# Windowed attention in blocks of 32 queries by 64 keys, with the mask added on VectorE and the maximum subtracted on GpSimd

## The chip, the cores and the metric

The kernel runs on one core of a Trainium2 chip. A core has five engines with queues of their own: TensorE (PE; its weight loads are shown as PEld), VectorE (DVE), ScalarE (ACT), GpSimd (POOL) and SyncE (SP), which here issues the transfers. Each engine takes its instructions in the order in which the program lists them, and waits where one needs another engine's result. The metric is the device time of one execution in microseconds (us).

## The reference

There are two parts, one after the other, for a batch of 8 sequences of 512 tokens with 128 features. The first part is one layer of causal attention with 16 heads of 8 features, whose weights are found by four Newton steps. It is not touched by the change.

The second part has six layers. Each computes queries, keys and values for 16 heads of 64 features, scales queries and keys to unit length, rotates them, and lets each query attend to its own window of 32 tokens and the 32 before it:

```python
mask = (it < jb) | (it > jb + w) | (jb == -1)          # w = 32
sim = jnp.einsum('bhwie,bhwje->bhwij', bq, bk2) * QK_SCALE
sim = jnp.where(mask, -jnp.finfo(sim.dtype).max, sim)
attn = jax.nn.softmax(sim, -1)
out = jnp.einsum('bhwij,bhwje->bhwie', attn, bv2)
```

The heads are joined by `Wo` and added to the input; a feed-forward block with layer norm, two projections, a GELU gate and a projection back follows, and is added too.

## The kernel before

All arithmetic is in float32. The second part is one long pipeline over *halves*: a half is one layer, one sequence and 8 of the 16 heads, and there are 6 × 8 × 2 = 96 of them. A half has four *pairs* of heads, so the loop `while t < ...` makes 384 steps of one pair each, with a few more at the ends. One step `t` of the loop holds work of several stages:

- `turn(a)` (L570) transposes the rotated queries and keys of pair `t` on PE, so that features lie on partitions; ACT copies them to `qT`.
- `share` (L614) sums the exponentials of the pair before over the keys (DVE, `rs`, L618), takes the reciprocal (L619), and multiplies by it on POOL (L620).
- `turn_weights` (L624) transposes the weights of the pair two steps back on PE, and ACT copies them to `prT` (L631).
- `prepare_qk` (L511) makes queries and keys for one quarter of the next half: the projection `m` on PE (L518), its squares on ACT (L523) and their sums `ss` on DVE (L524), and the rotation: two products on DVE (L526, L534), an add on POOL (L538), and after the reciprocal root of `ss` on ACT (L542, L543) a multiplication on POOL (L546).
- `weigh(a)` (L585) makes the scores of pair `t` and their exponentials; it is what the change rewrites.
- `gather` (L633) multiplies the weights of the pair two steps back with the values on PE (`po`), and ACT copies the result to `oT` (L647); `leave` (L649) multiplies it with `wo` into `acc`.
- `prepare_v` (L550) makes a quarter of the next half's values, which ACT copies into `v` (L558); after the fourth quarter `spread` (L560) moves `v` by transfers within on-chip memory to `v3`, where the keys of each query block lie on partitions.

In eight steps of two halves, the feed-forward block of one sequence runs in pieces between the stages: `gp` (L703), `ap` (L713) and `y` (L724) are its three groups of matmuls, and the GELU (L664) needs two loads of a function table around it.

In `weigh` a block has 64 queries and 96 keys. Two PE matmuls per pair (L592) first write the mask `band`, held in bfloat16, into PSUM with an identity matrix; 16 score matmuls (L601) add to it, in tiles of 64 rows by 64 columns. DVE takes the negative maximum (L607) and adds it (L608), for each of the two heads apart, straight from PSUM; ACT takes exp of both (L612). The weights of a pair are 128 partitions by 768 numbers.

The order of the instructions on each engine is made when the program is built, by a scheduler with a model of times; the engines keep to it. Buffers come from pools: `ps_a` has four PSUM banks that rotate through transposes, projections and the feed-forward block, `ps_b` two for the scores, `ps_c` one each for `po` and `acc`. `v` has one buffer, `v3` and most others two, `pr` three.

Of the kernel before, what the change touches and what calls it, by code (L numbers as in the profile page):

```python
# [16 lines left out]
P = 128  # L17
N = 512
# [14 lines left out]
WIN = 32  # L33
QB = 64
KB = QB + WIN
NQ = N // QB
HH = H // 2
HC = HH * DHL
# [11 lines left out]
def tile_kernel(  # L50
# [26 lines left out]
    make_identity(nc, ident)  # L77
    ident_h = const.tile([P, P], BF16, name="ident_h")
    nc.gpsimd.tensor_copy(ident_h, ident)
    eps_ln = const.tile([P, 1], F32, name="eps_ln")  # L80
# [349 lines left out]
    nc.gpsimd.memset(band[0:QB, 0, 0:WIN], NEG)  # L430

# [128 lines left out]
    def spread(g):  # L560

        v, v3 = g["v"], g["v3"]
        nc.gpsimd.memset(v3[0:WIN, 0, :], 0.0)
        for u in range(2):
# [20 lines left out]
    def weigh(a):  # L585

        qT = a["qT"]
        a["pr"] = pr = tp.tile([P, 2, NT, KB], F32, name="pr", bufs=3)
        nm = tp.tile([P, 2, NT], F32, name="nm")
        s = [ps_b.tile([P, NT, KB], F32, name="s2") for e in range(2)]  # L590
        for e in range(2):
            nc.tensor.matmul(  # L592
                s[e].rearrange("p c k -> p (c k)"), lhsT=ident_h,
                rhs=band.rearrange("p c k -> p (c k)"), start=True, stop=False,
            )
        for n in range(NQ):
            c, u = n // 2, n % 2
            k0 = max(n * QB - WIN, 0)
            for e in range(2):
                hr = slice(e * DHL, (e + 1) * DHL)  # L600
                nc.tensor.matmul(  # L601
                    s[e][u * QB : (u + 1) * QB, c, KB - (n + 1) * QB + k0 : KB],
                    lhsT=qT[0][hr, n * QB : (n + 1) * QB], rhs=qT[1][hr, k0 : (n + 1) * QB],
                    start=False, stop=(n >= NQ - 2),
                )
        for e in range(2):
            nc.vector.tensor_reduce(nm[:, e], s[e], axis=AX.X, op=ALU.max, negate=True)  # L607
            nc.vector.tensor_tensor(  # L608
                pr[:, e], s[e], nm[:, e].unsqueeze(2).to_broadcast([P, NT, KB]), ALU.add
            )  # L610
        flat = pr.rearrange("p e c k -> p (e c) k")
        nc.scalar.activation(flat, flat, AF.Exp)  # L612

    def share(a):  # L614

        flat = a["pr"].rearrange("p e c k -> p (e c) k")
        rs = tp.tile([P, 2 * NT], F32, name="rs")
# [5 lines left out]

    def turn_weights(a):  # L624
        pr = a["pr"]
        a["prT"] = prT = tp.tile([KB, 2, NT, P], F32, name="prT")
        for e in range(2):
            pT = ps_a.tile([KB, NT, P], F32, name="pT2", tag="mm")
            for c in range(NT):
                nc.tensor.transpose(pT[:, c, :], pr[:, e, c, :], ident)  # L630
            nc.scalar.copy(prT[:, e], pT)  # L631

    def gather(a):  # L633

        g, p, prT = a["g"], a["p"], a["prT"]
        po = ps_c.tile([P, N], F32, name="po2")
        for n in range(NQ):
            for e in range(2):
                h = 2 * p + e
                nc.tensor.matmul(  # L640
                    po[e * DHL : (e + 1) * DHL, n * QB : (n + 1) * QB],
                    lhsT=g["v3"][:, n, h * DHL : (h + 1) * DHL],
                    rhs=prT[:, e, n // 2, (n % 2) * QB : (n % 2 + 1) * QB],
                    start=True, stop=True,
                )
# [222 lines left out]
```

## Time and profile before

| quantity | value |
| --- | --- |
| median of three runs | 5278.99 us (5274.19 to 5279.23) |
| profiled execution | 5272.88 us |
| its span | 5271.2 us, so 1.7 us lie around it |
| DVE busy over the span | 4459.5 us (85%) |
| PE busy over the span | 4383.2 us (83%) |
| ACT busy over the span | 3831.5 us (73%) |
| POOL busy over the span | 3207.5 us (61%) |
| mean granted PE clock | 0.883 of full speed |

In a row of the profile, a group of instructions is named by its line, engine, operation, and tiles as `out<-in`; `x` gives how many there were, followed by busy time and mean length. A timeline row gives start, length, engine, line and tiles, and in brackets how long the engine stood idle before it and what ended the wait. In a row of the view by stretches, the stretch and its length come first, then busy time and number of instructions of PE, PEld, DVE, ACT and POOL, the granted PE clock, the share of time in which the transfer engines were busy, and GB/s. In the chain that ended last, each row has a start, a length and what the chain ran through; a chain that stays on one engine means that nothing else set the pace there.

### The profile page before, as it was taken

To read this page: it belongs to the slowest core of one execution; us is meant where nothing else is said; L and a number is where in the kernel's file an instruction comes from. 1 tells how busy PE (TensorE), PEld (TensorE's weight loads), DVE (VectorE), ACT (ScalarE), POOL (GpSimd) and SP (SyncE) were. 2 spreads that over 40 slices of the span, in tenths; PEclk is the share of its full clock that TensorE was granted. 3 is DMA by queue.
4 is the path that set the end of the run, shared out by engine and by line. 5 is a ranking of instruction groups with operands and counts; after the bars stand their busy time and mean duration, and the time that the engine had idled before them with its cause. 6 is when DMAs were issued, how large, how long until landed. Compare 5 with 4: busy or idle time off the path is not lost.

```text
span 5271.2 us, 116180 instructions
## 1 busy us (share of the span) xinstructions
PE 4383.2 (83%) x44173; PEld 2609.3 (50%) x44173; DVE 4459.5 (85%) x11788; ACT 3831.5 (73%) x6698; POOL 3207.5 (61%) x3919
## 2 busy tenths in 40 slices
PE   4555556556554799999999999999999999999998
PEld 1222222223222466666666666666666666666665
DVE  7888888888887788888888888888888888888886
ACT  6899888888889466666666666666666666666665
POOL 2444434444445677777777767777777777677674
PEclk7666666666665899999999999999999999999999
DMA  0000000000000211221112212121122112121221
GB/s 9 1 5 1 5 5 1 5 3 3 3 1 3 68 47 38 50 53 46 47 41 58 50 37 51 48 53 46 37 50 61 40 46 49 44 57 46 49 55 36
DMA packets 115043, 177.87 MB, mean 34 GB/s; under 512 B 13072, under 2 KB 38456, under 8 KB 114488
## 3 DMA queue, kind: packets, MB, share of 16 engines
q1 hardware_dynamic: 114488, 170.45, 13.0%
q8 instruction: 351, 5.75, 0.5%
q14 instruction: 204, 1.67, 0.1%
HBM read 21.52 MB, written 4.19 MB: 5 GB/s over the span
## 4 chain that ended last, share of the span: by engine, by line
DVE 40%; PE 33%; ACT 17%; POOL 6%; issue 3%; DMA 0%; SPq 0%; ACTq 0%; POOLq 0%; DVEq 0%
DVE stw L285 7%; DVE qr L534 6%; DVE ss L524 5%; PE m L518 5%; DVE qn L526 5%; ACT d L283 4%; ACT d L282 3%; DVE rs L618 3%; PE po L640 3%; PE pv L554 3%; PE pT L630 3%; PE acc L653 3%; PE s L601 2%; PE s L242 2%; PE y L724 2%
## 5 line engine op out<-in xcount | busy, mean ns | idle before, releaser
L538 POOL TENSOR_TENSOR qn<-qn,qr 128x512 f32<-128x512 f32 x768 | 974.5, 1269 | 458.9 <-DVE qr L534 326.3
L620 POOL TENSOR_TENSOR pr<-pr,rs 128x768 f32<-128x768 f32 x384 | 564.1, 1469 | 503.3 <-DVE rs L619 255.2
L285 DVE BATCH_NORM_STATS2 stw<-d 128x6 f32<-128x224 f32 (+15 forms) x2048 | 770.1, 427 | 115.9 <-ACT d L283 114.9
L257 POOL TENSOR_TENSOR d<-ns,lam 128x32 f32<-128x32 f32 (+7 forms) x1024 | 401.4, 426 | 729.3 <-DVE stw L285 229.6
L546 POOL TENSOR_TENSOR qn<-qn,ss 128x512 f32<-128x512 f32 x768 | 784.5, 1042 | 56.3 <-ACT ss L543 56.2
L518 PE MATMUL m<-wqkv,xs 128*128 128x512 f32 x1536 | 750.0, 606 | 79.6 <-ACT qT L582 67.8
L524 DVE TENSOR_REDUCE ss<-sq 128x8 f32<-128x512 f32 x768 | 521.2, 679 | 256.7 <-ACT sq L523 254.9
L282 ACT ACTIVATE d<-ns,lam 128x416 f32<-128x416 f32 (+7 forms) x1024 | 566.8, 614 | 36.6 <-DVE stw L285 14.8
L534 DVE TENSOR_TENSOR qr<-m,tab 128x256 f32<-128x256 f32 x1536 | 570.6, 412 | 0.0
L647 ACT COPY oT<-po 128x512 f32<-128x512 f32 x384 | 223.9, 583 | 461.3 <-PE po L640 461.2
L283 ACT ACTIVATE d<-d 128x1344 f32<-128x1344 f32 (+3 forms) x512 | 551.4, 1095 | 0.2
L242 PE MATMUL s<-kn,qj 32*32 32x352 f32 (+15 forms) x4096 | 422.5, 519 | 151.4 <-DVE mn L247 148.5
L526 DVE TENSOR_TENSOR qn<-m,tab 128x512 f32<-128x512 f32 x768 | 513.9, 669 | 0.0
L618 DVE TENSOR_REDUCE rs<-pr 128x8 f32<-128x768 f32 x384 | 363.6, 947 | 171.8 <-ACT pr L612 171.6
L323 PE MATMUL dTp<-ident,da 128*128 128x128 f32 x1280 | 303.2, 377 | 243.8 <-issue 95.7
L523 ACT ACTIVATE sq<-m 128x512 f32<-128x512 f32 x768 | 433.8, 602 | 82.7 <-PE m L518 67.7
L582 ACT COPY qT<-ptq 128x512 f32<-128x512 f32 x768 | 414.0, 583 | 83.8 <-PE ptq L577 78.8
L257 POOL TENSOR_TENSOR da<-ns,lam 128x416 f32<-128x416 f32 (+15 forms) x512 | 310.4, 639 | 259.2 <-PE dTp L323 229.0
L577 PEld LDWEIGHTS ptq<-ident,qn 128*128 128x128 f32 x3072 | 359.0, 141 | 219.4 <-issue 112.0
L640 PE MATMUL po<-prT,v 96*64 96x64 f32 x12288 | 443.2, 225 | 0.1
L631 ACT COPY prT<-pT 96x512 f32<-96x512 f32 x768 | 427.9, 587 | 13.2 <-PE pT L630 7.7
L554 PE MATMUL pv<-wqkv,xs 128*128 128x512 f32 x768 | 432.2, 645 | 0.9 <-PE m L518 0.7
(137 smaller groups left out, 8785.2 us busy)
## 6 DMA issues: line engine op xcount, KB each, us to landing
v<-v SPq DMA_DIRECT2D x192, 512.0 KB
v<-v SPq DMA_DIRECT2D x96, 256.0 KB
v<-v SPq DMA_DIRECT2D x96, 192.0 KB
wqkv<-in_L_ffn_Wqkv_dram SPq DMA_DIRECT2D x36, 256.0 KB
wo<-in_L_ffn_Wo_dram SPq DMA_DIRECT2D x12, 256.0 KB
xb<-in_L_attn_x_dram SPq DMA_DIRECT2D x8, 256.0 KB
x<-xb SPq DMA_DIRECT2D x8, 256.0 KB
xr<-x SPq DMA_DIRECT2D x8, 256.0 KB
```

Source lines behind the costliest of these rows:

```text
L257: nc.gpsimd.tensor_tensor(o, n, by.to_broadcast([P, keys(W, a)]), ALU.add)
L282: nc.scalar.activation(dv[a], nv[a], AF.Ln, bias=lam[:, c : c + 1])
L283: nc.scalar.activation(d, d, AF.Exp, scale=-1.0)
L285: nc.vector.bn_stats(st[:, 4 * j + a].rearrange("p u k -> p (u k)"), dv[a])
L518: nc.tensor.matmul(m.rearrange("p h e -> p (h e)"), lhsT=lhsT, rhs=wqkv[:, t, :], start=True, stop=True,)
L524: nc.vector.tensor_reduce(ss[:, t, :], sq, axis=AX.X, op=ALU.add)
L526: nc.vector.tensor_tensor(qc, m, tab[:, 2 * t, c, :].unsqueeze(1).to_broadcast([P, HH, DHL]), ALU.mult)
L534: nc.vector.tensor_tensor(qr[:, :, u, :], mh[:, :, 1 - u, :], sw.unsqueeze(1).to_broadcast([P, HH, hd]), ALU.mult,)
L538: nc.gpsimd.tensor_tensor(qc, qc, qr.rearrange("p h u e -> p h (u e)"), ALU.add)
L546: nc.gpsimd.tensor_tensor(qc, qc, ss[:, t, :].unsqueeze(2).to_broadcast([P, HH, DHL]), ALU.mult)
L554: nc.tensor.matmul(pv, lhsT=lhsT, rhs=wqkv[:, 2, :], start=True, stop=True,)
L640: nc.tensor.matmul(po[e * DHL : (e + 1) * DHL, n * QB : (n + 1) * QB], lhsT=g["v3"][:, n, h * DHL : (h + 1) * DHL], rhs=prT[:, e, n // 2, ...
```

## The change

A block now has 32 queries and 64 keys, and the scores of both heads of a pair lie in one PSUM tile of two banks. The mask no longer passes through PE: DVE adds `band`, now float32, to the scores as it moves them out of PSUM, for both heads in one instruction, and takes the maximum from the result; POOL adds the negative maximum. The first block of a sequence has 64 keys too, of which the mask takes away those that lie ahead, so `band` is built differently for it.

The two heads' weights lie side by side, 2 × 64 keys, so that one PE transpose of 128 columns turns both: four transposes and one ACT copy per pair instead of eight and two. The score matmuls have tiles of 64 rows by 32 columns and 64 keys, 32 of them per pair instead of 16. `gather` multiplies 64 keys with 32 queries, 32 matmuls per pair instead of 16, one head on the lower and one on the upper half of the partitions. So `v3` is laid out anew, and `spread` has 18 transfers in place of 4; the value columns of `wqkv` are loaded in an order that puts even heads first, with two transfers in place of one.

```diff
-QB = 64
+QB = 32
 KB = QB + WIN
 NQ = N // QB
+UB = P // QB
...
-    ident_h = const.tile([P, P], BF16, name="ident_h")
-    nc.gpsimd.tensor_copy(ident_h, ident)
...
-    ps_b = ctx.enter_context(tc.tile_pool(name="ps_b", bufs=2, space=PSUM))
+    ps_b = ctx.enter_context(tc.tile_pool(name="ps_b", bufs=1, space=PSUM))
...
-    band = k2.tile([P, NT, KB], BF16, name="band")
+    band = k2.tile([P, NT, KB], F32, name="band")
...
-    nc.gpsimd.memset(band[0:QB, 0, 0:WIN], NEG)
+    nc.gpsimd.memset(band[0:QB, 0], 0.0)
+    nc.gpsimd.affine_select(
+        out=band[0:QB, 0], in_=band[0:QB, 0], pattern=[[-1, KB]], base=0,
+        channel_multiplier=1, compare_op=ALU.is_ge, fill=NEG,
+    )
...
-        for k in range(3):
+        for k in range(2):
             c0 = k * INNER + hv * HC
             nc.sync.dma_start(w[:, k, :], f_wqkv[l][:, c0 : c0 + HC])
+
+        c0 = 2 * INNER + hv * HC
+        cols = f_wqkv[l][:, c0 : c0 + HC].rearrange("i (p e d) -> i e p d", e=2, d=DHL)
+        for e in range(2):
+            nc.sync.dma_start(
+                w[:, 2, e * (HC // 2) : (e + 1) * (HC // 2)].rearrange("i (p d) -> i p d", d=DHL),
+                cols[:, e],
+            )
...
-        v3 = vp.tile([KB, NQ, HC], F32, name="v3")
+        v3 = vp.tile([P, NQ, HC // 2], F32, name="v3")
...
     def spread(g):
         v, v3 = g["v"], g["v3"]
-        nc.gpsimd.memset(v3[0:WIN, 0, :], 0.0)
-        for u in range(2):
-            nc.sync.dma_start(v3[WIN:KB, u::2, :], v[u * QB : (u + 1) * QB])
-        nc.sync.dma_start(v3[0:WIN, 1::2, :], v[QB - WIN : QB])
-        nc.sync.dma_start(v3[0:WIN, 2::2, :], v[P - WIN : P, 0 : NT - 1])
+        for e in range(2):
+            at = slice(e * KB, e * KB + WIN)
+            cols = slice(e * (HC // 2), (e + 1) * (HC // 2))
+            for u in range(UB):
+                own = v[u * QB : (u + 1) * QB, :, cols]
+                c = 1 if u == 0 else 0
+                nc.sync.dma_start(v3[e * KB + WIN : (e + 1) * KB, u + c * UB :: UB, :], own[:, c:])
+                if u < UB - 1:
+                    nc.sync.dma_start(v3[at, u + 1 :: UB, :], own)
+                else:
+                    nc.sync.dma_start(v3[at, UB::UB, :], own[:, 0 : NT - 1])
+            nc.sync.dma_start(v3[e * KB : (e + 1) * KB, 0, :], v[0:KB, 0, cols])
...
     def weigh(a):
         qT = a["qT"]
-        a["pr"] = pr = tp.tile([P, 2, NT, KB], F32, name="pr", bufs=3)
-        nm = tp.tile([P, 2, NT], F32, name="nm")
-        s = [ps_b.tile([P, NT, KB], F32, name="s2") for e in range(2)]
-        for e in range(2):
-            nc.tensor.matmul(
-                s[e].rearrange("p c k -> p (c k)"), lhsT=ident_h,
-                rhs=band.rearrange("p c k -> p (c k)"), start=True, stop=False,
-            )
+        a["pr"] = pr = tp.tile([P, NT, 2, KB], F32, name="pr", bufs=3)
+        nm = tp.tile([P, NT * 2], F32, name="nm")
+        both = ps_b.tile([P, 2, N], F32, name="s2")
+        s = both[:, :, 0 : NT * KB].rearrange("p e (c k) -> p e c k", c=NT)
         for n in range(NQ):
-            c, u = n // 2, n % 2
+            c, u = n // UB, n % UB
...
-                    s[e][u * QB : (u + 1) * QB, c, KB - (n + 1) * QB + k0 : KB],
-                    lhsT=qT[0][hr, n * QB : (n + 1) * QB], rhs=qT[1][hr, k0 : (n + 1) * QB],
-                    start=False, stop=(n >= NQ - 2),
-                )
-        for e in range(2):
-            nc.vector.tensor_reduce(nm[:, e], s[e], axis=AX.X, op=ALU.max, negate=True)
-            nc.vector.tensor_tensor(
-                pr[:, e], s[e], nm[:, e].unsqueeze(2).to_broadcast([P, NT, KB]), ALU.add
-            )
-        flat = pr.rearrange("p e c k -> p (e c) k")
+                    s[u * QB : (u + 1) * QB, e, c, :],
+                    lhsT=qT[0][hr, n * QB : (n + 1) * QB], rhs=qT[1][hr, k0 : k0 + KB],
+                    start=True, stop=True,
+                )
+        nc.vector.tensor_tensor(
+            pr.rearrange("p c e k -> p e c k"), s,
+            band.unsqueeze(1).to_broadcast([P, 2, NT, KB]), ALU.add,
+        )
+        flat = pr.rearrange("p c e k -> p (c e) k")
+        nc.vector.tensor_reduce(nm, flat, axis=AX.X, op=ALU.max, negate=True)
+        nc.gpsimd.tensor_tensor(
+            flat, flat, nm.unsqueeze(2).to_broadcast([P, 2 * NT, KB]), ALU.add
+        )
         nc.scalar.activation(flat, flat, AF.Exp)
...
     def turn_weights(a):
         pr = a["pr"]
-        a["prT"] = prT = tp.tile([KB, 2, NT, P], F32, name="prT")
-        for e in range(2):
-            pT = ps_a.tile([KB, NT, P], F32, name="pT2", tag="mm")
-            for c in range(NT):
-                nc.tensor.transpose(pT[:, c, :], pr[:, e, c, :], ident)
-            nc.scalar.copy(prT[:, e], pT)
+        a["prT"] = prT = tp.tile([P, NT, P], F32, name="prT")
+        pT = ps_a.tile([P, NT, P], F32, name="pT2", tag="mm")
+        for c in range(NT):
+            nc.tensor.transpose(pT[:, c, :], pr[:, c].rearrange("p e k -> p (e k)"), ident)
+        nc.scalar.copy(prT, pT)

     def gather(a):
...
         for n in range(NQ):
+            c, u = n // UB, n % UB
             for e in range(2):
-                h = 2 * p + e
+                rows = slice(e * KB, (e + 1) * KB)
                 nc.tensor.matmul(
                     po[e * DHL : (e + 1) * DHL, n * QB : (n + 1) * QB],
-                    lhsT=g["v3"][:, n, h * DHL : (h + 1) * DHL],
-                    rhs=prT[:, e, n // 2, (n % 2) * QB : (n % 2 + 1) * QB],
+                    lhsT=g["v3"][rows, n, p * DHL : (p + 1) * DHL],
+                    rhs=prT[rows, c, u * QB : (u + 1) * QB],
                     start=True, stop=True,
                 )
```

More of the change, by code (lines that the diff above doesn't have):

```diff
@@ L562, in spread @@
         v, v3 = g["v"], g["v3"]
-        nc.gpsimd.memset(v3[0:WIN, 0, :], 0.0)
-        for u in range(2):
-            nc.sync.dma_start(v3[WIN:KB, u::2, :], v[u * QB : (u + 1) * QB])
-        nc.sync.dma_start(v3[0:WIN, 1::2, :], v[QB - WIN : QB])
-        nc.sync.dma_start(v3[0:WIN, 2::2, :], v[P - WIN : P, 0 : NT - 1])
+        for e in range(2):
+            at = slice(e * KB, e * KB + WIN)
+            cols = slice(e * (HC // 2), (e + 1) * (HC // 2))
+            for u in range(UB):
+                own = v[u * QB : (u + 1) * QB, :, cols]
[6 more added lines that the diff above has]
+            nc.sync.dma_start(v3[e * KB : (e + 1) * KB, 0, :], v[0:KB, 0, cols])
     def turn(a):
@@ L601, in weigh @@
                 nc.tensor.matmul(
[L602 to L611 removed]
+                    s[u * QB : (u + 1) * QB, e, c, :],
+                    lhsT=qT[0][hr, n * QB : (n + 1) * QB], rhs=qT[1][hr, k0 : k0 + KB],
+                    start=True, stop=True,
+                )
+        nc.vector.tensor_tensor(
[7 more added lines that the diff above has]
+        )
         nc.scalar.activation(flat, flat, AF.Exp)
     def share(a):
[L616 removed]
+        flat = a["pr"].rearrange("p c e k -> p (c e) k")
         rs = tp.tile([P, 2 * NT], F32, name="rs")
```

## The prediction

> **What bounds the kernel now.** I read the page first, then the second part by stretches, then the chain that ended last, then one step engine by engine. The change touches only the second part (about 1790 us to the end).
>
> ```profile
> PE 4383.2 (83%) x44173; PEld 2609.3 (50%) x44173; DVE 4459.5 (85%) x11788; ACT 3831.5 (73%) x6698; POOL 3207.5 (61%) x3919
> ```
> ```profile
> 400.00:800.00 400.00, 227.41 (x1936) 112.26 (x1936) 333.50 (x1191) 353.17 (x509) 166.84 (x366) 0.65 0.01 4
> ...
> 3000.00:5000.00 2000.00, 1952.54 (x20604) 1219.04 (x20603) 1741.07 (x3875) 1342.82 (x2619) 1421.83 (x1324) 1.00 0.19 48
> ```
> The page's averages mix two parts. In the second (last row), PE is busy 98%, DVE 87%, POOL 71%, ACT 67%, and the clock is full. Exp of L612 runs 342 times between 2100.3 and 5196.6 us, so one head pair (a "step") takes 3096.3/341 = 9.08 us.
>
> ```profile
> 3508.12 1.72 PE m L518 x4
> 3509.84 0.33 PE s L592 x2
> 3510.17 0.82 PE s L601 x32
> 3510.99 1.08 PE po L640 x32
> 3512.07 1.05 PE pv L554 x2
> 3513.12 2.58 PE y L724 x6
> 3515.70 0.86 PE acc L653 x2
> 3516.56 0.87 PE ptq L577 x8
> 3517.44 0.87 PE pT L630 x8
> ```
> The chain stays on PE for long stretches. Without feed-forward a step's PE work is 1.72+.33+.82+1.08+1.05+.86+.87+.87 = 7.6 us; `gp`, `ap`, `y` add 2.58 us in three steps of eight.
>
> A second loop lies just under it. Here are DVE's row sum and rotation, then its softmax work after them, then POOL and ACT beside it, from the timeline of one step without the 2.58 us matmuls (start, length):
> ```profile
> 3534.70 0.95 DVE L618 TENSOR_REDUCE rs<-pr 128x8 f32<-128x768 f32 x1 [0.97 <-ACT pr L612]
> 3535.67 0.69 DVE L524 TENSOR_REDUCE ss<-sq 128x8 f32<-128x512 f32 x1
> ...
> 3538.79 0.74 DVE L534 TENSOR_TENSOR qr<-m,tab 128x256 f32<-128x256 f32 x2
> ```
> ```profile
> 3539.52 1.01 DVE L607 TENSOR_REDUCE nm<-s 128x4 f32<-128x384 f32 x2
> 3540.45 1.01 DVE L608 TENSOR_TENSOR pr<-s,nm 128x384 f32<-128x384 f32 x2
> ...
> 3542.43 0.95 DVE L618 TENSOR_REDUCE rs<-pr 128x8 f32<-128x768 f32 x1
> ```
> ```profile
> 3539.67 1.27 POOL L538 TENSOR_TENSOR qn<-qn,qr 128x512 f32<-128x512 f32 x1 [0.37 <-DVE ss L541]
> 3540.91 2.04 POOL L546 TENSOR_TENSOR qn<-qn,ss 128x512 f32<-128x512 f32 x2
> ```
> ```profile
> 3541.56 0.84 ACT L612 ACTIVATE pr<-pr 128x768 f32<-128x768 f32 x1 [0.19 <-DVE pr L608]
> ```
> Call x the end of the last rotation product (3538.79+.74 = 3539.53). Then: subtraction ends x+1.93, exp ends x+2.87, the row sum `rs` starts x+2.90. `rs` stands in DVE's order ahead of the next step's rotation, and from `rs` to the next x is 3539.53−3534.70 = 4.83 us. Period 7.73 us: DVE and ACT go round in about PE's time, and POOL is not in this loop.
>
> **The change, part by part.** The kept rows give the prices; PE first, per step.
>
> *Mask matmuls* go: −.33. *Weight transposes* go from 8 to 4 of 128 columns at .109: −.43. *Scores*: 32 instructions on four tiles take .82; 64 on eight tiles, each tile 8 of 64 columns. Eight turns of 64/96 of today's .10 are about .55, plus start: .63, so −.19. If 64 cost what each of 32 costs now (25.6 ns): 1.64, +.82. *Gather*: 32 instructions, two tiles side by side, 1.08. Afterwards 64, moving 32 columns instead of 64, with weights of 64 columns as before. Weight loads average 133 ns for 64 columns (L601) and 190 for 128 (L518), .89 ns a column, so 64 columns need 57 ns, while 32 moving columns need 32 × .85 = 27 ns. The loads no longer hide: 32 turns × 57 + .15 = 1.97, +.89. Ends: hidden all the same 1.04 (−.04), or 64 at today's 33.7 ns, 2.16 (+1.08). PE sum: −.06 us a step, between −.99 and +1.14. Work on PE is about unchanged; matmuls are not where the time moves.
>
> *DVE* loses two reductions and two subtractions (1.93 together), gains an add from PSUM of 512 (as L526, .67, in steady turn .60) and a reduction (as L524, .68, in turn .60); row sum 768 to 512 saves .35. *ACT*: one copy of .58 goes, exp 768 to 512 takes about .60 (L523's 602 ns). *POOL* gains a broadcast subtraction of 128x512, the form of L546 (1042 ns), and its weighting falls from 1469 to 1042; the memset of .51 per half goes. POOL: about 6.45−.43−.13+1.04 = 6.9 us a step, not full.
>
> But the loop now passes through POOL, whose order in the built program is `qn`+`qr` twice, `qn`×`ss` twice, then the subtraction, then the weighting; only a few steps differ. From the rows above: second add x+.14, multiplications x+1.38 to x+3.42, subtraction x+3.38 to x+4.42. Mask add and maximum are done on DVE at x+1.3 and wait for nothing; the 2.0 us of multiplications, until now beside the loop, stand in it. Exp ends x+5.11, `rs` starts x+5.14; from `rs` to the next x 4.83−.35 = 4.48. What waits behind the subtraction on POOL, the weighting and the next adds, is not needed before the next x. Period **9.6 us** against PE's 7.6.
>
> ACT's order adds to it. Behind the waiting exp stand, in about 26% of steps, nothing that matters (9.61); in 36% the copy of `prT` (.48 in turn), which puts `ss` .37 behind the end of the row sum (9.98); in 26% both `qT` copies and `prT` (three × .48): exp ends x+5.11, `sq` to x+7.2, then 3.75 of DVE: 10.95; in 12% also the copy of `v`: 11.45. DVE cannot start `ss` without `sq`, nor PE the scores without `qT`. In one step of eight the copies of `xf` (.60+.61) stand before the subtraction: +1.24/8. Mean: .26×9.61+.36×9.98+.26×10.95+.12×11.45+.155 = 10.47 us. Feed-forward steps (PE 10.2) coincide with the late-exp ones and fit in them, and DVE's extra work there fits into its wait from x+1.3 to x+5.14.
>
> The subtraction against a page: the Trainium skill, "GPSIMD Engine Reference", section 3.1, has GpSimd taking 1.96 times as long as VectorE on a two-input add. Against the .67 of L526 that estimate gives 1.31 for the subtraction, .27 more a step, +104 us; the row of the same form here has 1042 ns, and the sum goes by the row.
>
> *Spread of v*: 18 transfers a half instead of 4, 2.0 MB instead of 1.5. Fourteen are issued after the last chunk of `v`, at the .62 to .67 us of L565 and L567: 9.8 us, and 2.5 more until the last lands. The next half's first copy into the single buffer `v` waits for it, and ACT behind it. Today that copy starts 11.8 to 13.0 us after the last; in the built order it stands one step with GELU or three steps later (16 us and more). So 0; without that cover up to 3 us × 48 = 144. `v3` is wanted four steps later. The split `wqkv` loads (12 in all) have five steps. The larger band is built once: +0 to 5 us. The scores keep two PSUM banks, single buffered as now, and give them back after one DVE add (x+.7) instead of after the second subtraction (x+1.9): no cost. A bank of the pool of four is held while a chunk of `v` waits for its copy, two steps at most in every other half; the transposes need one bank less a step, so I count 0, and up to 1 us × 48 if PE has to wait.
>
> *Sum.* (10.47−9.08) × 384 steps = +534 us on the profiled 5272.9, which lies 6.1 below the median shown: 5807, or about 5812 beside the median.
>
> **Rivals.**
> A. PE stays the bound: the loop is hidden, because POOL reaches the subtraction early (its 71% leaves room). Then −.06 × 384: about 5250, faster; with the best PE end 4900. It decides if POOL's chain ends before x+3.9, that is, if the multiplications do not stand ahead; the built order speaks against it.
> B. The loop holds but every step is like the best, 9.61 without late exp: +204, 5483.
> C. PE's clock falls too. In the first part PE is busy 57% and is granted .65 (row above); in the second 98% and 1.00. After the change PE has 7.5 to 8.5 us of work in 9.6 to 11, with gaps of one to three us. A third of the steps with one 3.4 us stretch at half clock (its records come in multiples of that) would cost 1.7 each: +220, 6030. With the upper PE end and the wait for `v` 6150.
> The Trainium skill, "TensorE: Matmul & The Clock Gate", Part 1, lets the clock fall after an idle window of about 3.4 us; by that alone gaps of three us would keep it and C would cost nothing, though no row of the second part shows it.
>
> **How the numbers follow.** Forecast 70% (5600 to 5960); C or the wait for `v` beyond that 14% (5960 to 6150); B and between 10% (5300 to 5600); A 5%; within the bound 1%. The range 5540 to 6060 leaves out A, most of B and the top of C, about 2 in 10. About 0.2% (11 us) is what this measurement can tell from no change: slower .94, same .01, faster .05.
>
> **What would show it.** The DVE row sum waits about 1.5 to 3 us a step for exp (now .97 at most in the row above); exp waits for POOL's subtraction; PE busy falls below 90% in the second part; gather about 1.9, scores .6 us a step; POOL near 70%. Wrong if the chain stays on PE, if the subtraction starts before x+2, if the copy into `v` waits for transfers, or if the clock row falls under 1.00.

## The result, and the profile after

The changed kernel takes 5911.15 us (median of four, 5902.34 to 5930.81) against 5278.15 us before: 1.1206 times as long, with a 95% interval of 1.1177 to 1.1235. That is +633 us where +534 was forecast. The profiled execution took 5907.95 us, of which the span is 5906.2.

Here are the first row of the page, and the second part by stretches: stretch, length, then busy time and instructions of PE, PEld, DVE, ACT and POOL, then PE's clock, the transfer engines' share and GB/s.

```profile
PE 4695.6 (80%) x66445; PEld 2837.9 (48%) x66445; DVE 4186.3 (71%) x11020; ACT 3534.5 (60%) x6314; POOL 3390.7 (57%) x4211
```
```profile
3000.00:5000.00 2000.00, 1796.42 (x28302) 1134.29 (x28300) 1351.45 (x2927) 992.00 (x2035) 1295.95 (x1263) 0.96 0.23 55
```

The page alone misleads: PE's busy time went up by 312 us, as if PE had more to do. The stretch says the opposite. PE is busy 90% (98% before), DVE 68% (87%), ACT 50% (67%), POOL 65% (71%), and the clock is 0.96. Nothing is full, so a chain of waits sets the pace. The costliest groups name two of its links; the columns are busy time and mean ns, then the idle time ahead of the group and what ended it:

```profile
L637 DVE TENSOR_REDUCE rs<-pr 128x8 f32<-128x512 f32 x384 | 263.3, 686 | 964.2 <-ACT pr L631 964.2
L631 ACT ACTIVATE pr<-pr 128x512 f32<-128x512 f32 x384 | 241.9, 630 | 956.0 <-POOL pr L628 956.0
```

DVE's row sum waits 964 us for exp, and exp 956 us for POOL's subtraction: 2.5 us a step each. In the kernel before, the row sum waited 172 us in all:

```profile
L618 DVE TENSOR_REDUCE rs<-pr 128x8 f32<-128x768 f32 x384 | 363.6, 947 | 171.8 <-ACT pr L612 171.6
```

The chain that ended last, in one step (start, length, what it ran through):

```profile
3605.36 1.04 POOL qn L558
3606.39 1.01 POOL pr L628
3607.42 0.64 ACT pr L631
3608.08 0.69 DVE rs L637
3608.77 0.59 DVE ss L536
...
3611.88 0.66 DVE qr L546 x2
3612.54 0.09 DVE ss L553
3612.63 0.05 issue
3612.69 0.48 POOL qn L550
3613.17 0.74 issue
3613.91 2.06 POOL qn L558 x2
3615.97 1.01 POOL pr L628
```

This is the forecast loop. One turn, from one subtraction (3606.39) to the next (3615.97), takes 9.58 us. The two multiplications L558 stand right ahead of the subtraction, although the subtraction needs nothing of them. The chain before ran along PE; PE is not in this turn at all.

The step with the GELU holds something else. This is its timeline on ACT and then PE (in brackets the idle time ahead of a row, and what ended it):

```profile
3650.74 1.28 ACT L684 ACT_TABLE_LOAD   x1
3652.04 1.49 ACT L684 ACTIVATE gate<-gate 128x1536 f32<-128x1536 f32 x1
3653.54 1.28 ACT L685 ACT_TABLE_LOAD   x1
...
3655.20 0.57 ACT L667 COPY oT<-po 128x512 f32<-128x512 f32 x1
3658.51 0.63 ACT L631 ACTIVATE pr<-pr 128x512 f32<-128x512 f32 x1 [2.74 <-POOL pr L628]
3659.05 0.57 ACT L570 COPY v<-pv 128x512 f32<-128x512 f32 x1
```
```profile
3656.33 1.02 PE L673 MATMUL acc<-oT,wo 128*128 128x512 f32 x2
3659.67 1.09 PE L597 MATMUL ptq<-ident,qn 128*128 128x128 f32 x8 [2.31 <-ACT v L570]
```

`pv` was ready at 3653.9, but its copy into `v` stands behind exp, and exp waits 2.74 us for POOL. The copy is what empties the PSUM bank that `ptq` wants, so PE stands still for 2.31 us, and the next step starts late.

Worked out from the times of DVE's `ss` maximum (L541 before, L553 after), and with the forecast's classes laid on the steps by what stands behind exp in ACT's order there, the mean lengths of the eight steps of a cycle are, in us:

| | 1 | 2 | 3 | 4 (GELU) | 5 | 6 | 7 | 8 | mean |
| --- | --- | --- | --- | --- | --- | --- | --- | --- | --- |
| before | 8.59 | 9.13 | 9.77 | 10.32 | 10.19 | 8.19 | 7.73 | 8.64 | 9.07 |
| forecast | 9.98 | 9.98 | 10.95 | 11.45 | 10.95 | 10.85 | 9.61 | 9.98 | 10.47 |
| after | 9.93 | 10.71 | 10.91 | 13.04 | 10.98 | 10.77 | 9.50 | 9.88 | 10.72 |

Six of eight are within 0.11 us. Steps 4 (+1.59) and 2 (+0.73) are not. Step 4 is the one above. In step 2 ACT still has three copies into `v` to make, ahead of and between the two instructions that make the reciprocal root `ss`. Here is one such step, of 10.50 us at full clock, whose last rotation product ends at x = 2948.45:

```profile
2948.52 1.08 ACT L570 COPY v<-pv 128x512 f32<-128x512 f32 x2
2949.47 0.24 ACT L554 ACTIVATE ss<-ss 128x16 f32<-128x16 f32 x1
2949.59 0.60 ACT L570 COPY v<-pv 128x512 f32<-128x512 f32 x1
2950.05 0.25 ACT L555 ACTIVATE ss<-ss 128x16 f32<-128x16 f32 x1
2950.44 2.05 POOL L558 TENSOR_TENSOR qn<-qn,ss 128x512 f32<-128x512 f32 x2 [0.63 <-ACT ss L555]
```

POOL's multiplications need `ss` and start at x+1.99, where x+1.38 was forecast; the subtraction, exp and `rs` come later by as much. In the mean of all steps 2 `rs` starts at x+5.90, in steps 1 at x+5.04.

### The profile page after: what moved, and what is told of

Read it like the earlier page. It is cut to its first block, busy times and chain, and to the rows that moved or that the text cites. A ratio compares the mean times of both kernels' runs of the same rounds, so it can differ in the third digit from the quotient of the medians.

```text
span 5906.2 us, 161419 instructions
## 1 busy us (share of the span) xinstructions
PE 4695.6 (80%) x66445; PEld 2837.9 (48%) x66445; DVE 4186.3 (71%) x11020; ACT 3534.5 (60%) x6314; POOL 3390.7 (57%) x4211
## 3 DMA queue, kind: packets, MB, share of 16 engines
q14 instruction: 205, 1.68, 0.1%
## 4 chain that ended last, share of the span: by engine, by line
DVE 30%; POOL 22%; ACT 20%; PE 20%; issue 7%; ACTq 0%; SPq 0%; DMA 0%; POOLq 0%; DVEq 0%
POOL qn L558 9%; DVE stw L284 6%; DVE qr L546 6%; POOL pr L628 6%; DVE ss L536 5%; DVE qn L538 5%; PE po L660 4%; POOL qn L550 3%; ACT d L282 3%; ACT pr L631 3%; PE m L530 3%; ACT d L281 3%; PE s L241 2%; POOL d L256 2%; PE dTp L322 2%
## 5 line engine op out<-in xcount | busy, mean ns | idle before, releaser
L637 DVE TENSOR_REDUCE rs<-pr 128x8 f32<-128x512 f32 x384 | 263.3, 686 | 964.2 <-ACT pr L631 964.2
L660 PE MATMUL po<-prT,v 64*64 64x32 f32 x24576 | 841.9, 222 | 108.2 <-ACT prT L650 102.0
L660 PEld LDWEIGHTS po<-prT,v 64*64 64x64 f32 x24576 | 797.5, 137 | 152.4 <-ACT prT L650 117.4
L530 PE MATMUL m<-wqkv,xs 128*128 128x512 f32 x1536 | 788.4, 629 | 99.4 <-ACT prT L650 59.2
L558 POOL TENSOR_TENSOR qn<-qn,ss 128x512 f32<-128x512 f32 x768 | 784.3, 1042 | 64.7 <-ACT ss L555 62.6
L631 ACT ACTIVATE pr<-pr 128x512 f32<-128x512 f32 x384 | 241.9, 630 | 956.0 <-POOL pr L628 956.0
L639 POOL TENSOR_TENSOR pr<-pr,rs 128x512 f32<-128x512 f32 x384 | 400.3, 1042 | 638.8 <-ACT sq L535 219.8
L536 DVE TENSOR_REDUCE ss<-sq 128x8 f32<-128x512 f32 x768 | 521.5, 679 | 264.8 <-ACT sq L535 258.6
L597 PE MATMUL ptq<-ident,qn 128*128 128x128 f32 x3072 | 433.5, 283 | 172.5 <-ACT v L570 109.3
L597 PEld LDWEIGHTS ptq<-ident,qn 128*128 128x128 f32 x3072 | 371.2, 147 | 412.3 <-issue 207.2
L566 PE MATMUL pv<-wqkv,xs 128*128 128x512 f32 x768 | 483.0, 714 | 9.8 <-DVE qr L546 4.4
```

The costliest lines, as they stand in the source:

```text
L530: nc.tensor.matmul(m.rearrange("p h e -> p (h e)"), lhsT=lhsT, rhs=wqkv[:, t, :], start=True, stop=True,)
L536: nc.vector.tensor_reduce(ss[:, t, :], sq, axis=AX.X, op=ALU.add)
L558: nc.gpsimd.tensor_tensor(qc, qc, ss[:, t, :].unsqueeze(2).to_broadcast([P, HH, DHL]), ALU.mult)
L597: nc.tensor.transpose(pt[:, c * P : (c + 1) * P], g["qn"][t][:, c, 2 * p : 2 * p + 2, :].rearrange("p h e -> p (h e)"), ident,)
L660: nc.tensor.matmul(po[e * DHL : (e + 1) * DHL, n * QB : (n + 1) * QB], lhsT=g["v3"][rows, n, p * DHL : (p + 1) * DHL], rhs=prT[rows, c, u ...
```

## Experiments

My theory is that the loss is the *latency* of a loop that POOL's order makes long, and not the work of any engine. The rivals are that PE's smaller tiles, POOL as a resource, the clock, or the transfers cause it by themselves.

### The subtraction back on VectorE

```diff
-        nc.gpsimd.tensor_tensor(
+        nc.vector.tensor_tensor(
             flat, flat, nm.unsqueeze(2).to_broadcast([P, 2 * NT, KB]), ALU.add
```


> The kernel after, with one word changed: VectorE instead of GpSimd subtracts the maximum. Blocks, tiles, transfers and the mask's place stay as in the kernel after. My theory (the loop through POOL sets the step): the loop leaves POOL. Three passes of some 0.68 us on DVE from x+0.14 end at x+2.2, exp of 0.63 ends at x+2.9, rs starts there as it did in the kernel before, and with 4.48 us behind it the loop is 7.4 us, below PE's work, which is 0.12 us a step more than before. The time falls to about 5320 us (5280 to 5380), and the wait of rs for exp to below 1 us a step. First rival (the small tiles of PE, the 18 transfers of spread or the clock's half-speed pieces cause the loss by themselves): it stays above 5700 us. Second rival (both have a part): 5450 to 5650 us.

Measured: 5372.96 us, 1.0185 (1.017 to 1.02), and `rs` waits 0.4 us a step for exp. The loss falls from 633 us to about 96, with all the blocks, tiles and transfers of the changed kernel in place. The first rival falls. One number of mine was wrong: the pass does not take 0.68 us on DVE. From the groups between 2100 and 5100 us, and the timeline of one step:

```profile
L628 DVE TENSOR_TENSOR pr<-pr,nm 128x512 f32<-128x512 f32 x322 | 451.8, 1403 | 6.8
L622 DVE TENSOR_TENSOR pr<-s,band 128x512 f32<-128x512 f32 x322 | 221.3, 687 | 0.0
```
```profile
3006.37 2.05 POOL L558 TENSOR_TENSOR qn<-qn,ss 128x512 f32<-128x512 f32 x2
3007.43 1.54 DVE L628 TENSOR_TENSOR pr<-pr,nm 128x512 f32<-128x512 f32 x1
3009.07 0.63 ACT L631 ACTIVATE pr<-pr 128x512 f32<-128x512 f32 x1 [1.49 <-DVE pr L628]
```

The add that reads scores from PSUM takes 687 ns; the subtraction, both of whose inputs lie in SBUF, takes 1403, more than POOL needs (1042). Of all 384, it averages 692 ns in the 27 cases in which POOL has nothing in hand when it starts, and 1451 ns in the 353 in which POOL is in L558 (the other four stand beside other work). In the row above it ends 0.55 us after POOL does. The Trainium skill, "SBUF — State Buffer", section "Who interferes with whom", says that a DVE instruction with two SBUF inputs contends with a GpSimd one that reads SBUF. These rows agree: the same subtraction takes about twice as long beside L558. So POOL's multiplications stood in the way on DVE as well, by about 0.7 us a step, but not for their full 2 us.

### Only the order on POOL

```diff
+    def scale_qk(g, ss, c):
         for t in range(2):
             qc = g["qn"][t][:, c]
             nc.gpsimd.tensor_tensor(
                 qc, qc, ss[:, t, :].unsqueeze(2).to_broadcast([P, HH, DHL]), ALU.mult
             )
...
-        nc.gpsimd.tensor_tensor(
+        a["sub"] = nc.gpsimd.tensor_tensor(
             flat, flat, nm.unsqueeze(2).to_broadcast([P, 2 * NT, KB]), ALU.add
...
         if a:
             weigh(a)
+        if ahead:
+            with tc.issue_after(a["sub"].ins) if a else nullcontext():
+                scale_qk(ahead, ss, c)
```
(`issue_after` puts what its block holds behind the named instruction in the queue of the same engine; it adds no wait.)

> The kernel after, with one order changed on POOL: the two multiplications of qn by ss, of 2.05 us together, stand behind the subtraction of the same step and no longer ahead of it. POOL does the same work in the same number of instructions. My theory (the loop is long since the subtraction stands behind the multiplications): the subtraction starts when the maximum is there, x+1.4, and ends near x+2.5, exp near x+3.2, and with 4.48 us behind rs the loop is 7.7 us, below PE's 8.7 to 9.2 us a step. The time falls to 5200 to 5430 us, with POOL as busy as before. Rival (what counts is the work that POOL has, or the crossing from DVE to POOL and back, wherever it stands in the order): above 5700 us. Between them, 5450 to 5650 us, if exp now waits for the copies ahead of it on ACT instead.

Measured: 5353.51 us, 1.0143 (1.0127 to 1.0158). Turning round three instructions on one queue takes away 558 of the 633 us. The subtraction still runs on POOL at 1043 ns. In its timeline the subtraction now starts with the maximum's end, and the multiplications run beside exp:

```profile
3007.33 0.69 DVE L631 TENSOR_REDUCE nm<-pr 128x8 f32<-128x512 f32 x1
3008.16 1.04 POOL L632 TENSOR_TENSOR pr<-pr,nm 128x512 f32<-128x512 f32 x1 [0.19 <-DVE nm L631]
3009.16 2.04 POOL L562 TENSOR_TENSOR qn<-qn,ss 128x512 f32<-128x512 f32 x2
3009.58 0.64 ACT L635 ACTIVATE pr<-pr 128x512 f32<-128x512 f32 x1
```
The same stretch as above, of this kernel:
```profile
3000.00:5000.00 2000.00, 1940.49 (x32662) 1276.23 (x32660) 1543.98 (x3355) 1161.21 (x2344) 1498.38 (x1457) 1.00 0.26 64
```
POOL is busier than in the changed kernel (75% against 65%), because the same work is done in less time; PE is back at 97%. DVE's order of products, sums and maximum is that of the changed kernel, and ACT's nearly so. POOL as a resource is out, and so is the crossing from DVE to POOL and back as such. The light step 7 takes 7.75 us here, the 7.7 us that the expectation gives the loop.

### A POOL pass in the kernel before

```diff
+    zero = k2.tile([P, 2 * NT], F32, name="zero")
+    nc.gpsimd.memset(zero, 0.0)
...
         flat = pr.rearrange("p e c k -> p (e c) k")
+        nc.gpsimd.tensor_tensor(
+            flat, flat, zero.unsqueeze(2).to_broadcast([P, 2 * NT, KB]), ALU.add
+        )
         nc.scalar.activation(flat, flat, AF.Exp)
```


> The kernel before, with a POOL pass over pr (128 x 768) that adds zeros, put between the subtraction on DVE and exp. It changes no number and no other instruction; blocks are 64 by 96 and the mask stays on PE. A pass of that shape takes 1.47 us (the weighting, L620 of the kernel before). My theory: it waits for the multiplications of qn until x+3.4, ends at x+4.9, exp of two heads ends near x+5.9, rs starts there in place of x+2.9, and the loop becomes 5.9+4.8=10.7 us against 9.08: at least +620 us, 5900 us, and to 6250 us if as many steps as in the kernel after also catch a copy behind exp. Rival (the blocks of 32 by 64 cause the loss, and a POOL pass is hidden): 5280 to 5400 us.

Measured: 5984.1 us, 1.1342 (1.1323 to 1.1361). The loss can be made in the old kernel by one POOL pass ahead of exp, with its old blocks, its mask on PE and its four transfers. A step takes 10.94 us in the mean. The groups show that the pass never waits for its input; it is its place in POOL's queue that makes it late:

```profile
L617 ACT ACTIVATE pr<-pr 128x768 f32<-128x768 f32 x384 | 323.7, 843 | 824.9 <-POOL pr L614 824.9
L614 POOL TENSOR_TENSOR pr<-pr,zero 128x768 f32<-128x768 f32 x384 | 563.6, 1468 | 4.2 <-PE gp L708 1.8
```

### Exp one step later, in two versions

```diff
-        a["pr"] = pr = tp.tile([P, NT, 2, KB], F32, name="pr", bufs=3)
+        a["pr"] = pr = tp.tile([P, NT, 2, KB], F32, name="pr", bufs=5)
...
-        nc.scalar.activation(flat, flat, AF.Exp)
+    def soften(a):
+        flat = a["pr"].rearrange("p c e k -> p (c e) k")
+        nc.scalar.activation(flat, flat, AF.Exp)
...
-    LAG = 2
+    LAG = 3
...
-        if 1 <= t < len(pairs) + 1:
-            share(pairs[t - 1])
...
         gelus()
+        if 1 <= t < len(pairs) + 1:
+            soften(pairs[t - 1])
         if a:
             weigh(a)
+        if 1 <= t < len(pairs) + 1:
+            share(pairs[t - 1])
```


> The kernel after, with the exponential of a pair issued one step later, behind the projections, the row sum after the scores of the next pair, one more step before the weights are used (LAG 3), and five buffers for pr in place of three. The subtraction stays on POOL, behind the multiplications, and every instruction keeps its size. My theory (the loss is the latency of the loop, not POOL's busy time): with a step to spare nothing of the next step waits for the subtraction, PE sets the pace, and the time is 5150 to 5380 us. Rival one (POOL as a resource, or the work of PE, is the bound): the time stays above 5700 us. Rival two (half of it): 5450 to 5650 us.

Measured: 5849.42 us, 1.1084 (1.1067 to 1.11), on the side of rival one, so taken by itself this run spoke against my theory. Its timeline shows why it tells nothing of latency:

```profile
3002.50 0.63 ACT L635 ACTIVATE pr<-pr 128x512 f32<-128x512 f32 x1 [3.42 <-POOL pr L628]
...
3003.17 0.69 DVE L641 TENSOR_REDUCE rs<-pr 128x8 f32<-128x512 f32 x1 [4.72 <-ACT pr L635]
3003.77 0.67 DVE L536 TENSOR_REDUCE ss<-sq 128x8 f32<-128x512 f32 x1
```
The scheduler put `rs` ahead of the next step's `ss` and products again (L641 before L536), whatever the place in the program. DVE waits 4.72 us there, and `rs` waits 1021 us for exp over the whole run. In most steps the intended change was not made. The second version writes the two orders out:

```diff
+            g["square"] = nc.scalar.activation(sq, m, AF.Square)
...
+                g["product"] = nc.vector.tensor_tensor(
                     qr[:, :, u, :], mh[:, :, 1 - u, :],
...
+        past = pairs[t - 1] if 1 <= t < len(pairs) + 1 else None
+        if past:
+            with tc.issue_after(ahead["square"].ins) if ahead else nullcontext():
+                soften(past)
         if a:
             weigh(a)
+        if past:
+            with tc.issue_after(ahead["product"].ins) if ahead else nullcontext():
+                share(past)
```


> The kernel after with the exponential one step later, as in the run before it of that kind, but with two orders written out: exp stands behind the squares of the next step on ACT, and the row sum rs behind the products of the next step on DVE. In the run before it rs still stood ahead of those products in most steps, so the products still waited for the subtraction and the loop was as long as ever (10.4 us from x to x near 3007 us). The subtraction stays behind the multiplications on POOL. My theory (the loss is that DVE's products wait behind rs): DVE goes from the maximum straight to the next products, its own work of some 6.9 us is its period, and PE sets the pace with 8.7 to 9.2 us a step: 5130 to 5350 us. Rival (POOL's or PE's own work, or the clock, bounds it): above 5700 us.

Measured: 5375.76 us, 1.0183 (1.0168 to 1.0198). Here POOL's order is the changed kernel's, multiplications first, and most of the loss is gone all the same, since in most steps nothing on DVE waits for the subtraction any more (`rs` waits 121 us for exp in all, where it waited 964). It ends 26 us above the range that I gave: the lightest steps take 7.7 to 8.0 us, so the loop is gone from them, but the longest takes 12.07.

### The step with the GELU

```diff
-        v = vp.tile([P, NT, HC], F32, name="v", bufs=1)
+        v = vp.tile([P, NT, HC], F32, name="v", bufs=2)
```


> The kernel after, with two buffers for v in place of one. The copies of pv into v may then be placed earlier on ACT, as they need not wait for the spread of the half before. My theory on the part that the prediction left out (in the step with the GELU, PE's transposes wait 2.3 us for the bank of pv, since its copy into v stands behind exp on ACT): the loop through POOL is as it was, so the time stays near 5900 us, and falls by up to 75 us (48 steps of 1.5 us) to 5835 us where the copies move ahead of exp; where the copy of the GELU step stays behind exp it falls by less than 20 us. Rival (the order of ACT around v has no part in the loss): within 10 us of the kernel after, and the wait of ptq for the copy into v as long as before.

Measured: 5864.69 us, 1.1118 (1.1102 to 1.1135). It is 46 us less, but not for my reason: the copy of the GELU step stayed behind exp, PE's wait for it did not shrink (99.6 us in the changed kernel and 105.8 here, between 2100 and 5700 us), and that step even took 14.03 us. As a test of the GELU step this run is inconclusive. It does test step 2, which fell from 10.71 to 9.51: with two buffers the three copies into `v` no longer stand ahead of `ss` there, and POOL's multiplications start when the add before them is done (3014.89 + 1.27):

```profile
3014.93 0.21 ACT L554 ACTIVATE ss<-ss 128x16 f32<-128x16 f32 x1 [1.77 <-DVE ss L553]
3015.17 0.22 ACT L555 ACTIVATE ss<-ss 128x16 f32<-128x16 f32 x1
3016.12 2.05 POOL L558 TENSOR_TENSOR qn<-qn,ss 128x512 f32<-128x512 f32 x2
```

The next run moves the one copy of the GELU step:

```diff
+        turned = bool(waiting)
...
         if a:
-            weigh(a)
+            flat = weigh(a)
+            if not turned:
+                nc.scalar.activation(flat, flat, AF.Exp)
...
+            copied = prepare_v(ahead, wq[ahead["hv"]], c)
...
+        if a and turned:
+            with tc.issue_after(copied.ins) if ahead else nullcontext():
+                nc.scalar.activation(flat, flat, AF.Exp)
```


> The kernel after, with one order changed on ACT, in the step that has the GELU alone (one of eight): the copy of pv into v stands ahead of exp and no longer behind it. My theory (the GELU step's 13.0 us, where 11.45 was forecast, are PE's transposes waiting 2.3 us for the PSUM bank that this copy must empty): the copy runs while ACT waits for the subtraction, near 3 us earlier, PE's next step starts earlier, and the time falls by 0.9 to 1.5 us in each of 48 steps, 45 to 75 us, to 5835 to 5870 us; the wait of ptq for the copy into v, 134 us in the profile after, goes below 30 us. Rival (that step ends with the softmax loop, and PE's wait lies beside it): within 10 us of the kernel after, as PE then waits as long for something else.

Measured: 5800.43 us, 1.0992 (1.0974 to 1.101), 111 us less than the changed kernel; I had expected 45 to 75. On ACT the copy now runs at once behind `oT`, and exp waits alone; PE's wait for that copy is down from 42 cases and 99.6 us to 4 cases (from the waits between 2100 and 5700 us; total, times, longest; the 134 us of the expectation are the same wait of the weight loads, which falls to 10.7):

```profile
3610.19 0.59 ACT L570 COPY v<-pv 128x512 f32<-128x512 f32 x1
3613.04 0.63 ACT L829 ACTIVATE pr<-pr 128x512 f32<-128x512 f32 x1 [2.26 <-POOL pr L628]
```
```profile
PE ptq L597 <- ACT v L570: 2.6, 4, 1.6
```
Step 4 falls from 13.04 to 11.07 us, so 48 × 1.97 = 95 us of it lie there, and no other step moves by more than 0.2. The clock has a part in this. In the changed kernel 13 of 43 of these steps hold 3.41 us at half clock and take 13.78 us in the mean; the 30 at full clock take 12.75. With the copy moved none of them holds such a piece. So the copy alone is worth 1.68 us a step, 81 us, and up to 0.3 us a step is the clock, which no run sets apart.

### Looking for a better kernel

Two more runs have the late exp (with one more step of lag and five buffers for `pr`), and three add two orders to it: exp ahead of the GELU, and the feed-forward pieces of a step ahead of its scores:

```diff
-    def prepare_qk(g, wqkv, tab, c):
+    def prepare_qk(g, wqkv, tab, c, past=None):
...
+        if past:
+            with tc.issue_after(g["square"].ins):
+                soften(past)
         gelus()
...
         gelus()
+        parts = [n for n in parts if next(n, n) is not n]
         if a:
             weigh(a)
```

The kernel before with the late exp alone, the edit of the section on the late exp made to it:

> The kernel before (blocks of 64 by 96, mask on PE, subtraction on DVE) with the exponential one step later and rs behind the next step's products, as in the kernel after with a late exp. Theory: the kernel before, too, loses part of its 9.08 us a step to its loop through exp, since PE has 8.57 us of work a step: the time falls by up to 190 us, to 5090 to 5230 us. Rival (PE alone sets the pace of the kernel before and the loop is hidden): 5260 to 5290 us.

Measured: 5357.2 us, 1.0146 (1.0129 to 1.0163): slower, against the theory and outside the rival's range too. Its light steps fell (7.41 to 8.05 us where the kernel before has 7.73 to 8.64), but step 5 rose from 10.19 to 13.31.

The kernel before with the change's mask and subtraction, and the late exp. The first block takes 96 keys, with a mask and a transfer of `v` to match:

```diff
-            nc.tensor.matmul(
-                s[e].rearrange("p c k -> p (c k)"), lhsT=ident_h,
-                rhs=band.rearrange("p c k -> p (c k)"), start=True, stop=False,
-            )
...
+        nc.vector.tensor_tensor(
+            pr, s, band.unsqueeze(1).to_broadcast([P, 2, NT, KB]), ALU.add,
+        )
+        flat = pr.rearrange("p e c k -> p (e c) k")
+        nc.vector.tensor_reduce(nm, flat, axis=AX.X, op=ALU.max, negate=True)
+        nc.gpsimd.tensor_tensor(
+            flat, flat, nm.unsqueeze(2).to_broadcast([P, 2 * NT, KB]), ALU.add
+        )
```

> Blocks of 64 by 96 as in the kernel before, but with the change's mask (added by VectorE as the scores leave PSUM, one instruction for both heads), its one maximum, its subtraction on POOL, and with the late exp and row sum. The first block takes 96 keys, masked, so that nothing unwritten is read. PE loses the mask matmuls, 0.33 us a step, and has no small score and gather tiles: about 8.24 us a step. POOL has 6.3+1.5=7.8 us, DVE about 7.7. Theory (the change's parts are worth their PE time once nothing waits in the loop): 4960 to 5150 us. Rival (three engines near 8 us a step cannot be kept together): 5200 to 5400 us.

Measured: 5403.51 us, 1.0235 (1.022 to 1.025), just above the rival's range. The lightest steps take 7.3 us, which is the 7.6 us of PE's work before less the 0.33 of the mask, yet the heavy ones take up to 12.94. With the two orders, first this kernel:

> Blocks of 64 by 96 with the mask added on VectorE, the subtraction on POOL and the late exp, as in the run before it, with two orders changed: exp stands ahead of the GELU, and the feed-forward pieces of a step are issued ahead of its scores. In that run the light steps took 7.3 to 7.6 us, below the 7.7 to 8.6 us of the kernel before, but the step with the GELU took 12.9 us (the exp waited 4 us for the GELU and its table loads, rs for the exp) and the others with feed-forward matmuls near 11, where PE waited for banks that the gate on DVE still held. Theory: without these waits the heavy steps fall by 1 to 3 us each, and the time to 5050 to 5250 us. Rival (the stalls only move to other steps): 5300 to 5420 us.

Measured: 5328.76 us, 1.0093 (1.0076 to 1.011). Better by 75 us, and still behind the kernel before; a stall of 3 us moved to another step (11.28 us), as the rival said. Then the changed kernel:

> The kernel after with the late exp and row sum, and the same two orders: exp ahead of the GELU, the feed-forward pieces ahead of the scores. Theory: PE sets the pace in every step, 8.7 us in the mean, and the time falls from 5376 to 5150 to 5300 us. Rival (the stalls only move): 5330 to 5400 us.

Measured: 5435.12 us, 1.0295 (1.028 to 1.031), slower by 59 us than without the two orders, and outside both ranges. DVE waits 757 us for `sq` in it between 2100 and 5150 us; why is open. Then the kernel before:

> The kernel before with the late exp and row sum, and the same two orders. It tells apart what the orders bring (this run against the one before it of that kind, 5357 us) from what the change's blocks and its mask on VectorE bring (the other two runs of this set against this one). Theory: PE's work of 8.57 us a step sets the pace: 5100 to 5280 us. Rival (the stalls only move): 5320 to 5380 us.

Measured: **5195.97 us, 0.9838 (0.9824 to 0.9853): faster than both kernels**, by 84 us (1.6%) against before. None of the change is in it, only order, with the buffers and the lag that it needs: late exp, row sum behind the products, exp ahead of the GELU, feed-forward ahead of the scores. The late exp alone had made this kernel slower; which of the other two orders brought the gain is not shown. The same stretch shows PE busy 99% (98% before), with DVE at 88%:

```profile
3000.00:5000.00 2000.00, 1988.84 (x21055) 1250.45 (x21054) 1767.10 (x3973) 1380.99 (x2684) 1456.25 (x1354) 1.00 0.20 49
```

Among the three with the same orders the kernel before's blocks win by 133 us over the mask on DVE, and by 239 us over the changed kernel.

## Why the prediction was right, and where it was not

**The loop through POOL** was right in mechanism and size. `rs` was forecast at x+5.14; in the step at x = 3603.04 it starts at 3608.08, x+5.04. The subtraction was forecast at x+3.38 and starts at x+3.35. Over all steps but 2 and 6 the means by step are x+5.04 to x+5.32 and x+3.31 to x+3.59; in step 6 the copies of `xf` come first, as forecast. Two runs that take the multiplications out of the loop, by POOL's order and by DVE's, leave 1.4% and 1.8% of the 12%; one that puts a POOL pass into the old loop makes 13%.

**ACT's order classes** held: six of eight steps are within 0.11 us of the forecast.

**The term that failed** is "a bank of the pool of four is held while a chunk of `v` waits for its copy ... so I count 0, and up to 1 us × 48 if PE has to wait". PE does wait. Step 4 lies 1.59 us above its forecast, 76 us in 48 such steps, and 1.30 us (62 us) where the clock is full; the upper end of 48 us was too low as well. The forecast let this copy delay ACT alone, by the 0.5 us between 10.95 and 11.45, and that is a part of the 1.68 us that moving it gave back. It overlooked the way on. In the step shown the copy has its input from 3653.9 on; ACT has a table load and `oT` to finish until 3655.8, and from there to 3659.05 the copy only stands behind exp. PE needs the bank for `ptq` and makes `m` of the next step after it, so the squares and `ss` of that step are late as well. The GELU itself, with 4 us on ACT, matters less: it puts the subtraction at x+3.59 in the mean, 0.2 us behind the forecast.

**A second term at nothing**: for the single buffer of `v` the forecast counted 0, since the copies into it stand late enough in the order. In the changed kernel none of them waits for a transfer, so the 18 transfers of `spread` cost nothing by themselves, as forecast. But three copies stand so late that they come ahead of `ss` in step 2, which lies 0.73 us above its forecast, 35 us in all; with two buffers this step takes 9.51 us. Steps 4 and 2 are together 111 us over the forecast and the other six 17 us under it, which gives the gap of 99 us (633 less 534) to within 5 us.

**Rival C** (the clock falls too): a clock row under 1.00 was among the signs of being wrong, and it came, with 0.95 to 0.96. Its price did not, 220 us in the forecast. Besides the 13 GELU steps (13.78 us against 12.75) three steps 2 near the end hold 6.8 us at half clock and take 13.4 us where 10.50 is the rule, and steps 3 take 10.98 with such a piece and 10.80 without. All steps 1 hold pieces, and are as long as forecast; steps 8 take 9.88 us with and without. That is less than 30 us in all, and no run isolates it. The clock was 1.00 again in the run with POOL's order turned, with nothing done for the clock.

**PE's terms**: scores .63 forecast, .79 measured (3650.02 to 3650.81); gather 1.97 forecast, 1.99 measured (3650.81 to 3652.80); both are the medians over all steps too. The transposes of the weights halved, as said. So the sum was about +.1 us a step and not −.06. Hidden in the changed kernel, this can be some 45 of the 74 to 96 us by which the repaired ones still trail; the rest may lie in their steps with feed-forward work (10.95 us in step 4 against 10.32 with POOL's order turned) and is open.

**The page on GpSimd** (the Trainium skill, "GPSIMD Engine Reference", section 3.1): by its ratio of 1.96 the estimate for the subtraction was 1.31 us. On POOL the subtraction measured 1041 to 1043 ns in these kernels, as the row that the sum used; DVE took 692 ns for it with POOL idle, so the ratio here is 1.5.

## What to carry to other kernels

An operation that moves to another engine takes that engine's queue with it. What it costs is not only its own length (1.04 us here) but also all that stands ahead of it there and was harmless so far (2.05 us), if it lies in a loop from step to step. Read the built order before the price list; and where such a loss shows, try the order first: one turned pair on POOL gave back 558 of 633 us, and order, with the buffers for it, took 84 us off a kernel in which PE was busy 98%. The two orders that helped there made the changed kernel with the late exp 59 us slower, so each kernel needs its own trial.

A place in the program is not a place in the queue. The first run with exp "one step later" kept the changed kernel's loop in most steps, since the scheduler put `rs` back; compare the order in the trace with the one meant before a result is believed.

## What the runs showed of the hardware

- DVE's subtraction with both inputs in SBUF took 692 ns with POOL idle at its start, and 1451 ns while POOL multiplied (the run with the subtraction on VectorE).
- PE's clock fell to half in pieces of 3.41 us and multiples: 94 pieces, 380 us, between 1800 us and the end of the changed kernel, against two at the end of the kernel before. PE had not been idle for long: between 1800 and 5750 us it had no gap above 2.57 us, and in the 3.41 us ahead of the 89 pieces there its longest gap was 1.04 us in the median, and as little as 0.51. The Trainium skill, "TensorE: Matmul & The Clock Gate", Part 1, has the clock fall after an idle window of about 3.4 us, and tells farther on in that part of a kernel whose clock swung with short idle times between groups of matmuls. The length of the pieces agrees with the window; the idle times here are of the short kind.
- 64 matmul instructions (two for each of the program's) with weights of 64 columns and 32 moving columns took 1.99 us where 32 with 64 moving columns took 1.08, so 31 against 34 ns each: halving the moving columns saved almost nothing. The forecast's price, one weight load of 57 ns for two tiles side by side, gave 1.97.
